# Issuing the stores of the spectral result from ScalarE, with the order of all steps set anew

## The chip, the core and the metric

The kernel runs on one core of a Trainium2 chip. The metric is device time in microseconds (us), the median of several runs. Its engines are TensorE (PE in the profile; its weight loads are PEld), VectorE (DVE), ScalarE (ACT), GpSimd (POOL) and SyncE (SP). SP computes nothing here: it issues DMA transfers, in order. Each engine works through its own list of instructions in order and waits on semaphores for the others.

## The reference

32 images of 56 x 56 places with 96 channels go through two layers. Cut to what matters:

```python
# layer 0: layer norm, product to 192 channels, 3x3 convolution, SiLU, residual
h = layernorm(x);  y = conv3x3(h @ w_in[:, :192]) ;  x = x + silu(y)
# layer 1, first half: spectral mixing over the 3136 places of an image
h = relu(bn1(layernorm(t) @ w1.T))                     # 96 -> 192 channels
X = fft(h, axis=places)
xr = relu(X.real*rd - X.imag*idg + rb);  xi = relu(X.imag*rd + X.real*idg + ib)
t = t + bn2(ifft(xr + 1j*xi).real @ w2.T)              # 192 -> 96 channels
# layer 1, second half: two linear layers with 8-bit floating-point inputs
t = t + q_linear(relu(q_linear(layernorm(t), W1, b1)), W2, b2)
```

## The kernel before, in words

All images go through one long chain of *steps*, and four stages of four neighbouring images run side by side. While an image is in the spectral stage, the next ones are in the convolution and in the first transform, and an older one is in the last two linear layers. Image 19's input is read while image 15's spectral result is on its way back.

The Fourier transform over 3136 places is done as a transform over 56 rows and one over 56 columns, with data turned round between them by way of memory. For each image:

- `fetch`, `take_in`, `make_image`: four chunks of the input (`xl`, three buffers) are loaded (L404), their statistics taken on VectorE (`st_a`, L144), scaled (`xa`, L454) and multiplied into the convolution's input `img` (`im`, L180). `load` reads the same input once more into `t` for the residual (also L404).
- `conv_part` (`cv`, L215 and L219), `conv_tokens` (`st`, L253), `conv_end`: the convolution, turned back to places and added to `t`. `norm_b` takes the statistics of `t` (`st_b`, also L144), `deviation` finishes them, `tokens_a` transposes (`tp_n`, L172).
- `forth` (`ph`, L266), `forth_a` (`pa`, copied to `u` at L280), `store_a`: the product to 192 channels and the first transform. `u` is stored to memory in seven groups, `da<-u` (L506).
- `fetch_a` loads it turned round, `at<-da` (L512). The first three loads of an image wait for the last store of `da`.
- `second` (`px`, L294; ScalarE makes `av` from it, L299 to L301), `second_parts` and `second_relus` (`sv` and `gt` on VectorE, L310 to L320), `second_w2` (`pg`), `second_back` (`pe`, L347, copied by ScalarE to `es`, L349): the second transform, the mixing, the product to 96 channels and the first inverse transform.
- `store_back` stores `es` to memory, `de<-es` (L543): seven calls for an image, each of two DMAs, so 14 for an image and 448 in all. The seventh call is the last unit of an image; it is called es(3,0) below.
- `fetch_y` loads that turned round, `y<-de` (L552). The first of these loads needs all 14 stores. `back` (`py`, L191) and `back_end` do the second inverse transform and add to `t` (L560).
- `normal`, `ffn_start`, `ffn_first` (`pf`, L373, copied to `h` at L375), `ffn_middle` (L379, L383), `ffn_second` (`po`, L393, copied to `y` at L395), `ffn_end` (L400), `store` (`out<-t`, L606): the linear layers.

The order of the steps is written as a list: `plan` gives every step of every image a time, in units of an eighth of an image, and `SHIFT` adds a small correction by step name and arguments. The list is sorted by these times. A scheduler then simulates the program in that order and settles how the instructions of neighbouring steps interleave on each engine. So `SHIFT` decides what stands behind what on every engine and in SP's list.

All these transfers are issued by SP; only four loads at the start come from ScalarE. The completion of transfers is counted by eight semaphores that are used in turn, so a transfer also waits, before it is issued, until the one eight places earlier in the program has landed.

```python
    def store_back(im, m, j0):
        p0, p1 = UNITS[m]
        es = im.held.pop(("es", m, j0))
        rows = im.de[p0:p1].rearrange("(h j) m c -> m h j c", h=2)
        for half in range(2):
            nc.sync.dma_start(rows[:, half, j0 : j0 + 2], es[:, half])
```

Of the kernel before, what the change touches and what calls it, by code (L numbers as in the profile page):

```python
# [50 lines left out]


SHIFT = {
    "back": 0.016, "back_end": -0.049, "conv_end": 0.319, "conv_end:2:1": 0.035, "conv_first": 0.24,
    "conv_first:0": -0.152, "conv_last": 0.284, "conv_part": 0.25, "conv_part:1:0": -1.292, "conv_part:2:1": 0.03,
    "conv_tokens": 0.24, "conv_tokens:0:1": -0.118, "conv_tokens:1": -0.08, "deviation": 0.071,
    "deviation:1": -0.023, "fetch": 0.364, "fetch_a": 0.059, "fetch_a:3": 0.296, "fetch_a:4": 0.619,
    "fetch_a:5": 0.174, "fetch_y": 0.167, "fetch_y:6": 1.932, "ffn_end": -0.036, "ffn_end:5": 0.211,
    "ffn_first": -0.312, "ffn_first:0:1": 0.338, "ffn_first:1": 0.027, "ffn_first:2": 0.021,
    "ffn_first:2:1": -0.304, "ffn_first:3:2": -0.175, "ffn_middle": -0.085, "ffn_middle:1:1": -0.102,  # L60
    "ffn_middle:2": 0.023, "ffn_middle:5": -0.011, "ffn_middle:6": -0.156, "ffn_middle:6:2": 0.223,
    "ffn_second": -0.087, "ffn_second:2": 0.003, "ffn_start": -0.085, "forth": 0.014, "forth:0": 0.016,
    "forth:5:0": 0.224, "forth:5:1": -0.073, "forth_a": 0.013, "load": 0.179, "make_image": 0.24,
    "make_image:0:4": 0.012, "norm_b": 0.24, "normal": 0.071, "normal:1:0": -0.209, "normal:2:2": 0.065,
    "normal:6:0": -0.106, "second": 0.046, "second_back": 0.046, "second_back:0:0": -0.061, "second_back:1": -0.034,
    "second_back:2:2": 0.039, "second_parts:0:0": -0.03, "second_parts:1:0": -0.059, "second_parts:1:2": 0.22,
    "second_parts:2:1": 0.016, "second_parts:2:2": 0.11, "second_relus": -0.027, "second_relus:0:0": 0.092,
    "second_relus:0:1": -0.147, "second_relus:1:1": 0.116, "second_relus:1:2": 0.038, "second_relus:2:0": 0.003,
    "second_w2": 0.046, "second_w2:2": 0.01, "store": -0.085, "store:3": 0.36, "store:4": 0.04, "store:6": -0.25,
    "store_a": 0.016, "store_a:2": 0.657, "store_back": 0.077, "store_back:1:2": -0.126, "store_back:2": 0.123,  # L70
    "take_in": 0.376, "tokens_a": 0.014,
}


# [16 lines left out]
def hybrid_kernel(ctx: ExitStack, tc: tile.TileContext, x, par, spar, cpar, w_in, conv_w, w1, w2, fw1, fb1, fw2, fb2, fa, fb, ib, ia, rows, ones6, out):  # L91
    nc = tc.nc
# [445 lines left out]
    def store_back(im, m, j0):  # L538
        p0, p1 = UNITS[m]
        es = im.held.pop(("es", m, j0))  # L540
        rows = im.de[p0:p1].rearrange("(h j) m c -> m h j c", h=2)
        for half in range(2):
            nc.sync.dma_start(rows[:, half, j0 : j0 + 2], es[:, half])  # L543

    def fetch_y(im, g):
        if g < NG:
# [68 lines left out]
    def plan(b):  # L615
# [76 lines left out]
        for m, (p0, p1) in enumerate(UNITS):  # L692
            both = p1 - p0 > PG
            for at, u in ((0, 0), (0.606, 1), (1.099, 2)) if both else ((0.088, 0), (0.674, 2)):
                at += S0 + SS * m + (0.125 if m + u == 0 else 0)
                put(at, second, m, u)
                put(at + 0.22, second_parts, m, u)
                put(at + 0.47, second_relus, m, u)
            for j0 in range(0, (p1 - p0) // 2, 2):
                at = S0 + SS * m + (2.024 if both else 1.221) + 0.062 * j0  # L700
                put(at, second_w2, m, j0)
                put(at + 0.2, second_back, m, j0)
                put(at + 0.575, store_back, m, j0)
# [338 lines left out]
```

## Time and profile before

| what | value |
|---|---|
| median of 3 runs | 3087.11 us (3083.41 to 3087.77) |
| the profiled execution: its time, its span | 3088.49 us, 3086.4 us |
| busy share of the span: PE, PEld, DVE, ACT, POOL | 95%, 74%, 74%, 72%, 21% |
| mean granted clock of TensorE | 0.965 of full speed |
| bytes moved, mean rate | 363.65 MB, 118 GB/s |
| stores `de<-es` | 448, of 84 KB |
| loads `y<-de` / `at<-da` / `t<-in_x` (large) / `xl<-in_x` (large) | 224 of 168 KB / 224 of 336 KB / 96 of 360 KB / 93 of 360 KB |

"Granted clock" is the share of its full clock that TensorE was allowed at a time. Busy shares are averages: what matters is which wait ends last where TensorE stands idle. In the profile, a row with SPq or ACTq is a DMA instruction on the list of SP or ScalarE: its duration is the time for which it held that list, not the time of the transfer. Times in a view count from the start of the span; one image takes about 93 us, and the views below show the end of the spectral stage of one of them, around 1500 to 1530 us.

### The profile page before, as it was taken

To read this page: it belongs to the slowest core of one execution; us is meant where nothing else is said; L and a number is where in the kernel's file an instruction comes from. 1 tells how busy PE (TensorE), PEld (TensorE's weight loads), DVE (VectorE), ACT (ScalarE), POOL (GpSimd) and SP (SyncE) were. 2 spreads that over 40 slices of the span, in tenths; PEclk is the share of its full clock that TensorE was granted. 3 is DMA by queue.
4 is the path that set the end of the run, shared out by engine and by line. 5 is a ranking of instruction groups with operands and counts; after the bars stand their busy time and mean duration, and the time that the engine had idled before them with its cause. 6 is when DMAs were issued, how large, how long until landed. Compare 5 with 4: busy or idle time off the path is not lost.

```text
span 3086.4 us, 86223 instructions
## 1 busy us (share of the span) xinstructions
PE 2926.7 (95%) x34037; PEld 2298.6 (74%) x34037; DVE 2296.3 (74%) x6704; ACT 2237.1 (72%) x5415; POOL 644.2 (21%) x400
## 2 busy tenths in 40 slices
PE   8899999999999999999999999999999999999986
PEld 6678777778777778777777777777777777777764
DVE  5557777787777777777777777777777877776777
ACT  3467777778777778777777777777777777777876
POOL 2211122222122222122212122212122222121110
PEclk9899999999999999999999999999999999999996
DMA  4544355444354544354544454543455544444442
GB/s 95 148 108 100 100 134 134 125 123 112 99 136 129 128 123 106 105 139 127 128 116 105 116 139 126 129 114 103 120 132 125 127 122 105 119 124 108 111 112 61
DMA packets 500059, 363.65 MB, mean 118 GB/s; under 512 B 346156, under 2 KB 450636, under 8 KB 499428
## 3 DMA queue, kind: packets, MB, share of 16 engines
q1 hardware_dynamic: 497758, 357.39, 45.4%
q8 instruction: 268, 4.39, 0.6%
q10 hardware_dynamic: 1897, 0.76, 0.1%
q14 instruction: 136, 1.11, 0.1%
HBM read 201.13 MB, written 156.89 MB: 116 GB/s over the span
## 4 chain that ended last, share of the span: by engine, by line
PE 69%; DMA 13%; ACT 9%; DVE 7%; issue 1%; SPq 1%; POOL 0%; ACTq 0%; POOLq 0%; DVEq 0%
PE cv L219 12%; PE ph L266 8%; PE px L294 8%; PE pe L347 5%; PE im L180 5%; PE pg L337 4%; PE pa L191 4%; DMA xl<-in_x 4%; PE pg L333 4%; DMA de<-es 4%; PE cv L215 3%; PE py L191 3%; PE pf L373 3%; PE st L253 3%; DMA y<-de 2%; PE po L393 2%
## 5 line engine op out<-in xcount | busy, mean ns | idle before, releaser
L219 PE MATMUL cv<-img,wv 97*32 97x196 f32 x13248 | 658.3, 340 | 0.0
L219 PEld LDWEIGHTS cv<-img,wv 97*32 97x32 f32 x13248 | 427.7, 112 | 121.6
L154 POOL TENSOR_TENSOR rs_c<-var_c,mhalf 120x8 f32<-120x8 f32 (+1 forms) x128 | 209.7, 1639 | 1206.0 <-DVE var_c L152 1202.4
L294 PEld LDWEIGHTS px<-fb_sb,at 112*64 112x64 f32 (+1 forms) x3584 | 327.3, 173 | 121.6 <-issue 49.0
L266 PE MATMUL ph<-w1a,n2t 97*120 97x192 f32 x1792 | 399.1, 346 | 0.0
L268 ACT ACTIVATE h<-ph,rs_b 120x192 f32<-120x192 f32 x896 | 333.3, 432 | 84.2 <-PE ph L266 83.0
L294 PE MATMUL px<-fb_sb,at 112*64 112x112 f32 (+3 forms) x3584 | 388.7, 289 | 5.8 <-ACT y L395 1.9
L266 PEld LDWEIGHTS ph<-w1a,n2t 97*120 97x120 f32 x1792 | 288.6, 187 | 106.3 <-issue 64.0
L375 ACT CAST h<-pf 128x448 f16<-128x448 f32 x672 | 354.2, 554 | 8.4 <-PE pf L373 8.3
L154 POOL TENSOR_TENSOR rs_b<-var_b,mhalf 120x8 f32<-120x8 f32 (+1 forms) x128 | 233.2, 1831 | 537.0 <-DVE var_b L152 523.6
L154 POOL TENSOR_TENSOR rs_a<-var_a,mhalf 120x8 f32<-120x8 f32 (+1 forms) x128 | 198.2, 1550 | 657.4 <-DVE var_a L152 657.4
L180 PE MATMUL im<-rows_sb,xa 120*96 120x168 f32 x1792 | 325.1, 312 | 3.2 <-DVE xa L454 0.5
L379 DVE TENSOR_SCALAR h<-h,b1q 128x448 f16<-128x448 f16 x672 | 219.1, 331 | 107.0 <-ACT h L375 96.2
L312 ACT ACTIVATE sv<-sv 128x224 f32<-128x224 f32 (+2 forms) x352 | 138.8, 394 | 211.8 <-DVE sv L311 211.7
L299 ACT ACTIVATE av<-px,spar_sb 128x224 f32<-128x224 f32 (+2 forms) x352 | 161.0, 457 | 163.4 <-PE px L294 160.5
L180 PEld LDWEIGHTS im<-rows_sb,xa 120*96 120x96 f32 x1792 | 255.2, 164 | 23.9 <-ACT img L185 12.8
L310 DVE SCALAR_TENSOR_TENSOR sv<-px,spar_sb,av 128x224 f32<-128x224 f32 (+2 forms) x352 | 153.4, 436 | 153.5 <-ACT av L301 153.0
L144 DVE BATCH_NORM_STATS2 st_a<-xl 120x6 f32<-120x192 f32 x434 | 142.1, 355 | 163.1 <-DMA xl<-in_x 163.1
L337 PE MATMUL pg<-w2x,gt 128*112 128x96 f32 (+1 forms) x1792 | 246.2, 261 | 0.0
L373 PE MATMUL pf<-n3t,w1q 96*128 96x448 fp8e5 x672 | 231.1, 362 | 15.2 <-ACT n3t L368 7.8
L337 PEld LDWEIGHTS pg<-w2x,gt 128*112 128x112 f32 (+1 forms) x1792 | 244.3, 180 | 0.1
L333 PE MATMUL pg<-w2y,gt 128*112 128x192 f32 (+1 forms) x896 | 234.0, 343 | 4.5 <-DVE gt L320 2.8
(124 smaller groups left out, 6305.2 us busy)
## 6 DMA issues: line engine op xcount, KB each, us to landing
da<-u SPq DMA_DIRECT2D x448, 168.0 KB
at<-da SPq DMA_DIRECT2D x224, 336.0 KB
out<-t SPq DMA_DIRECT2D x224, 180.0 KB
de<-es SPq DMA_DIRECT2D x448, 84.0 KB
y<-de SPq DMA_DIRECT2D x224, 168.0 KB
t<-in_x SPq DMA_DIRECT2D x96, 360.0 KB
xl<-in_x SPq DMA_DIRECT2D x93, 360.0 KB
t<-in_x SPq DMA_DIRECT2D x32, 180.0 KB
```

The costliest lines, as they stand in the source:

```text
L154: nc.gpsimd.tensor_tensor(rs, var, mhalf[:, :n], ALU.pow)
L180: nc.tensor.matmul(ps[:, j], xa[:, t0 + j, :], rows_sb, start=True, stop=True)
L191: nc.tensor.matmul(to, lhs, rhs, start=True, stop=True)
L219: tc.keep_in_program_order(nc.tensor.matmul(*args, start=(dx == 0), stop=(dx == 2)))
L266: nc.tensor.matmul(ph[:, j, :], n2t[:, 2 * j2 + j, :], w1a, start=True, stop=True)
L268: nc.scalar.activation(h[:, j], ph[:, j % 2], AF.Relu, scale=rs[:, j : j + 1])
L294: nc.tensor.matmul(px[rows, j], lhs, fb_sb[:, first(p) : first(p + 1)], start=True, stop=True)
L333: nc.tensor.matmul(pg[:, :, j, :], lhs, w2y, start=True, stop=False, skip_group_check=True)
L337: nc.tensor.matmul(pg[:, half, j, :], lhs, w2x, start=False, stop=True, skip_group_check=True)
L373: nc.tensor.matmul(pf, w1q[:, k * 128 : (k + 1) * 128], n3t, start=True, stop=True)
L375: nc.scalar.copy(h1, pf)
L379: nc.vector.tensor_scalar(h2[:, k], h1, b1q[:, k : k + 1], 0.0, ALU.add, ALU.max)
```

## The change

The two DMAs of `store_back` are issued from ScalarE's list instead of SP's. The table `SHIFT` is replaced by a longer one, made with the assumption that transfers land later; through it the order of all steps changes. No arithmetic, tile or transfer is added or removed. In the new file all lines behind the table stand 12 lower (L543 becomes L555).

```diff
-    "back": 0.016, "back_end": -0.049, "conv_end": 0.319, "conv_end:2:1": 0.035, "conv_first": 0.24,
...
-    "deviation:1": -0.023, "fetch": 0.364, "fetch_a": 0.059, "fetch_a:3": 0.296, "fetch_a:4": 0.619,
-    "fetch_a:5": 0.174, "fetch_y": 0.167, "fetch_y:6": 1.932, "ffn_end": -0.036, "ffn_end:5": 0.211,
...
-    "forth:5:0": 0.224, "forth:5:1": -0.073, "forth_a": 0.013, "load": 0.179, "make_image": 0.24,
-    "make_image:0:4": 0.012, "norm_b": 0.24, "normal": 0.071, "normal:1:0": -0.209, "normal:2:2": 0.065,
...
-    "second_w2": 0.046, "second_w2:2": 0.01, "store": -0.085, "store:3": 0.36, "store:4": 0.04, "store:6": -0.25,
-    "store_a": 0.016, "store_a:2": 0.657, "store_back": 0.077, "store_back:1:2": -0.126, "store_back:2": 0.123,
-    "take_in": 0.376, "tokens_a": 0.014,
+    "back": 0.027, "back_end": -0.049, "back_end:2": -0.057, "conv_end": 0.41, "conv_end:0:1": 0.519,
...
+    "conv_tokens:2:1": -0.249, "deviation": -0.063, "deviation:1": -0.023, "fetch": 0.436, "fetch:3": 0.682,
+    "fetch_a": 0.033, "fetch_a:3": 0.249, "fetch_a:4": 0.619, "fetch_a:5": 0.174, "fetch_a:6": -0.088,
+    "fetch_y": 0.125, "fetch_y:4": 0.481, "ffn_end": -0.001, "ffn_end:2": 0.033, "ffn_end:3": 0.262,
...
+    "forth_a:3": -0.063, "load": -0.208, "load:2": 0.605, "make_image": 0.171, "make_image:0": 0.002,
+    "make_image:0:4": 0.012, "make_image:1:4": -0.429, "make_image:2": 0.06, "make_image:2:4": 0.003,
+    "norm_b": 0.233, "norm_b:0": -0.002, "norm_b:1": 0.517, "norm_b:2": 0.512, "normal": 0.011, "normal:0:0": 0.097,
...
+    "second_w2": 0.075, "second_w2:0:0": -0.023, "second_w2:2": 0.01, "store": -0.222, "store:3": 0.041,
+    "store:4": 0.04, "store:6": -0.25, "store_a": -0.165, "store_a:2": 0.657, "store_a:3": 0.064,
+    "store_back": 0.106, "store_back:0": 0.038, "store_back:1:2": -0.126, "store_back:2": 0.123,
+    "store_back:2:0": -0.125, "store_back:2:2": 0.567, "take_in": 0.236, "tokens_a": 0.075,
+    "tokens_a:3": -0.08,
...
-            nc.sync.dma_start(rows[:, half, j0 : j0 + 2], es[:, half])
+            nc.scalar.dma_start(rows[:, half, j0 : j0 + 2], es[:, half])
```

The instruction lists of the two built programs show what this does at the end of an image's spectral stage. Before, SP's list there reads: last store of `u`, `out`, `xl` chunk 1, three loads `at`, two loads `t`, `xl` chunk 2, the two stores of es(3,0), `out`, `xl` chunk 3, four loads `y`. After, it reads: two `out`, last store of `u`, two loads `t`, three loads `at`, `xl` chunks 1 and 2, `out`, `xl` chunk 3, four loads `y`. The two stores stand in ScalarE's list, each behind one more copy than the one that makes `es`. TensorE's list between `pe` of es(3,0) and `py` has nearly the same work in both. On VectorE, the statistics of `xl` chunk 1 stood ahead of the scaling of the next image's chunk 0 and well ahead of `sv` of the next image's first unit; after, three of their four instructions stand between that scaling and `sv`. Thirteen of the fourteen passes `st_b` stood ahead of `ffn_end` of group 3 on VectorE; after, all fourteen stand behind it.

## The prediction

> **What bounds the kernel now.** I read the page's busy shares first, then TensorE's waits, then SP's list and the chain around the largest wait, then rows by window.
>
> ```profile
> PE 2926.7 (95%) x34037; PEld 2298.6 (74%) x34037; DVE 2296.3 (74%) x6704; ACT 2237.1 (72%) x5415; POOL 644.2 (21%) x400
> ...
> PE py L191 <- DMA y<-de: 81.9, 31, 3.9
> PE ps_wt L751 <- DMA win<-in_w_in: 8.1, 1, 8.1
> PE st L253 <- ACT s L245: 8.1, 29, 1.4
> ```
>
> TensorE is the bound: 95% busy, no other engine above 74%. Of its waits (us in total, times, longest) only one is large: `py` waits 31 times for `y`, 81.9 us, so 2.64 us for an image. All others are below 0.3 us for an image. One image of the 31 (SP's rows, then the chain, each with start and duration):
>
> ```profile
> 1507.62 4.66 SPq L404 DMA_DIRECT2D xl<-in_x  x1
> 1512.33 0.90 SPq L543 DMA_DIRECT2D de<-es  x2
> 1513.32 0.50 SPq L606 DMA_DIRECT2D out<-t  x1
> ...
> 1518.03 2.01 SPq L552 DMA_DIRECT2D y<-de  x4
> ```
>
> ```profile
> 1508.71 0.47 ACT es L349
> ...
> 1512.77 5.21 DMA de<-es
> ...
> 1518.40 3.47 DMA y<-de
> ```
>
> The last `es` is ready at 1509.18, but its two stores stand in SP's list behind an `xl` load whose issue alone held the list 4.66 us. They go out at 1512.33, 3.15 us late; the landing takes 5.21 us, `y` another 3.47, and `py` starts at 1521.91 after a gap of 3.29 us. The gap has a second price:
>
> ```profile
> 1505.00:1509.00 4.00, 4.00 (x43) 3.97 (x42) 1.99 (x8) 2.61 (x7) 0.91 (x2) 1.00 0.94 271
> 1509.00:1514.00 5.00, 5.00 (x42) 4.91 (x39) 3.89 (x8) 4.68 (x13) 1.28 (x1) 1.00 1.12 197
> 1514.00:1517.00 3.00, 3.00 (x44) 2.49 (x46) 0.45 (x2) 3.00 (x10) 0.00 (x0) 1.00 1.02 263
> 1518.62:1521.91 3.29, 0.00 (x0) 0.00 (x0) 3.29 (x13) 0.00 (x0) 0.58 (x1) 1.00 0.68 192
> 1522.00:1529.00 7.00, 7.00 (x60) 4.24 (x64) 5.31 (x16) 2.75 (x7) 1.98 (x2) 0.51 0.65 184
> ```
>
> The three columns at the end are granted clock, DMA share and GB/s. Behind the gap the clock is 0.51 for 7 us. Behind two gaps of 2.20 us I found 0.72 (1708 to 1714) and 1.00 (2452 to 2458): a gap of that size may or may not cost the clock. From 216 to 2820 us, the steady part with 28 images, the mean clock is 0.98: 0.02 x 2604 = 52 us lost, 1.9 us for an image. So 2.64 + 1.9 = 4.5 us of an image hang on `y`. Also seen: before the gap the DMA engines are full (share 0.94 to 1.12).
>
> **The change part by part**, for one image, against the profiled 3088.49 us (1.4 above the median).
>
> A, the stores leave SP. They can go at 1509.7, behind the copy that follows `es` in ScalarE's list (ended 1509.65). With the old landing, 5.21 us, and 0.9 us for the two issues, `de` is complete at 1515.8. By then SP must also have come to its `y` loads; a first `y` issued at 1516 lands 3.8 us later, near 1519.8. Alone, this leaves 1.2 us of the 3.29; but TensorE arrives later too (C, D, E: 3.1 us in this image), at 1521.7. So the wait for `y` goes: -2.64. It stays at its old size if ScalarE's issue is stuck as SP's was.
>
> B, the clock. If the gap breaks into pieces of 2.1 us and less, most of the 1.9 comes back; the two gaps of 2.20 us say that some pieces still cost it. Bounds 0 and 1.9; I take three quarters, -1.4.
> [...]
>
> C, given back on VectorE. In the new order two `t` loads and three `at` loads stand ahead of chunk 1 of `xl`, and three of the four `st_a` of that chunk stand ahead of `sv` of the next image's first unit. In the old order this chunk was issued at 1503.11, ahead of `at`, and its `st_a` ran at 1506.89. Counted in the trace's packets, `t` (1920 packets at 440 for a us) takes 4.4 us, `at` (336 at 80) 4.2, `xl` (120 at 80) 1.5: 10.1 us from about 1504.2, and 0.8 us to the wake-up: 1515.1. Three `st_a` (0.89) and three `sv` passes (1512.92 to 1514.09, 1.17) make 1517.1. `px_0_1` on TensorE, which needs the buffer that the third pass frees, ran at 1515.00. So TensorE stands 2.1 us; scaled by 2.64 / 3.29 for a mean image +1.7. Bounds: 0, if `t` gets out 2 us sooner; 2.6, if the 2.09 MB go at 197 GB/s, the lowest full-share row above (10.6 us).
>
> D, `st_b` later. `deviation` must be done before `tp_n` in the middle of TensorE's work there. Its last steps cost VectorE 0.61 us for POOL's `rs_b` and 0.17 of its own (1505.59): between 0, if other work covers it, and 0.8; I take the middle, +0.4.
>
> E, fourteen issues on ScalarE. SP's rows of this form have a median of 0.447 us; ScalarE's own at the start of the kernel took 0.23 to 0.67. All 14: 6.3 us of ScalarE, which is idle for 28% of 93 us. The pair of es(3,0) delays `av` by 0.9 us, where ScalarE was busy 4.68 of 5.00, but `sv` waits longer for `xl` there (C covers it; uncovered, the whole 0.9 would count). Of es(1) four stand in a row, 1.8 us; the 10 us around them (1560 to 1570) had 1.18 idle on ScalarE, so 0.6 is left. Bounds 0 and 1.8; +0.6. Queued behind each issue are `img`, `h` and `av` copies, for which TensorE waits through PSUM. All lane waits of these stores but one are long satisfied; that one, the second store of es(3,0), waits for the first `t` load, eight places earlier, whose packets are served first (done at 1504.2 + 2.2): no cost if `t` starts as in C.
>
> The other moved steps exchange neighbours on engines with 26% to 28% idle and keep TensorE's list nearly the same between `pe` and `py`: 0 taken; below nothing too, since the small waits of TensorE, some 60 us in all, may shrink or grow by a third (20 us either way).
>
> Sum: -2.64 - 1.4 + 1.7 + 0.4 + 0.6 = -1.34 us, times 31 = -42. 3088.5 - 42 = 3047, on the scale of the median 3046. Its own range, with C at 0 to 2.6 and the 20 us: 3010 to 3080.
>
> **The rivals.** (1) *All of it gained*: nothing of C, D, E reaches TensorE, as in the image above the old waits for VectorE and ScalarE were near zero. -2.64 - 1.9 = -4.54, times 31 = -141: 2946. For it: stores 3 us earlier are nearly the whole gap. Against it: A alone leaves 1.2 us, and without TensorE's delay `y` would still be late. Chance 0.13.
>
> (2) *Slower: ScalarE is held by its own issue.* The 4.66 us row shows that an issue can hold its list while the DMA engines are full (1.12 from 1509 to 1514). If SP's and ScalarE's issues share what is full, the first store, reached at 1509.7, goes when SP's did, at 1512.28: 2.6 us in which ScalarE stands, with `h`, `img` and `av` behind it; the second adds some 0.4. TensorE runs dry (it had no slack in `img` and `px`): +3.0 in place of C, +0.4 and +0.6 as before, `y` -2.64, and the clock is lost as now. +1.36 times 31 = +42: 3129. It decides once the two rows of es(3,0) hold ScalarE over 0.9 + 1.34 = 2.2 us for an image. For it: SP's row; against it: SP's list may have been stuck in a limit of its own, and the store is small beside `xl`. Chance 0.35.
> [...]
>
> (3) *No change*: the bytes ahead are the same, the engines are full until 1517, so `de` and `y` land when the backlog is through, whoever issues; the gap moves to other instructions and the clock drops as before. 3080 to 3100. For it: shares of 0.94 to 1.12; against it: from 1518.62 the share is 0.68, so the end of the gap is latency. Chance 0.16, half of it within 0.2%.
>
> **How the numbers follow.** Forecast 0.36, rivals 0.13, 0.35, 0.16. 0.2% (6 us) is what a measurement of this kernel can tell. Faster: 0.36 + 0.13 + 0.03 of rival 3 = 0.52; same 0.08; slower 0.35 + 0.05 = 0.40. Range: it leaves out half of rival 1 (below 2960) and a third of rival 2 (C on top of the held issue, above 3140), 0.18 together: 2960 to 3140. The forecast's own range is 3010 to 3080.
>
> **What would show it.** In the waits of TensorE, `py` for `y` should fall from 81.9 to below 20 us (A). The granted clock from 216 to 2820 us should be 0.99 or more (B). New waits: `px` for `sv` some 50 us, with VectorE's `st_a` held by `xl` ahead of it (C); `tp_n` some 12 us (D). ScalarE's issue rows should be near 0.45 us each (E); pairs of 2 us or more in front of `av` show rival 2. If `py` still waits 50 us with short issues, rival 3 holds. I am wrong in the mechanism if `py` waits less and another wait on TensorE, not named here, is over 30 us.

## The result, and the profile after

The changed kernel takes 3095.2 us (median of 5 runs, 3088.7 to 3104.3) against 3087.1 before: 1.0044 times, 95% interval 1.0026 to 1.0063, so slower by 0.4% and not faster. The forecast was 3046.

```profile
PE 2952.1 (96%) x34037; PEld 2299.8 (74%) x34037; DVE 2306.0 (75%) x6704; ACT 2261.1 (73%) x5415; POOL 616.7 (20%) x400
```

Busy time of the engines after: TensorE is busy 25 us longer for the same instructions. Its waits:

```profile
PE px L306 <- DVE sv L325: 51.0, 29, 2.9
PE py L203 <- DMA y<-de: 12.3, 8, 3.9
```

`py` waits 12.3 us in place of 81.9, as forecast; `px` waits 51.0 for `sv`, also as forecast. The image that matches the one shown of before, first in SP's list, then in ScalarE's:

```profile
1502.49 0.95 SPq L416 DMA_DIRECT2D t<-in_x  x2
1503.87 1.46 SPq L524 DMA_DIRECT2D at<-da  x3
1505.38 0.88 SPq L416 DMA_DIRECT2D xl<-in_x  x2
...
1517.30 1.60 SPq L564 DMA_DIRECT2D y<-de  x4
```

```profile
1508.40 0.48 ACT L361 COPY es<-pe 112x384 f32<-112x384 f32 x1
...
1508.91 0.31 ACTq L555 DMA_DIRECT2D de<-es  x1
...
1509.29 0.44 ACTq L555 DMA_DIRECT2D de<-es  x1
```

ScalarE issues the first of the two stores 0.03 us behind the last `es`; the issues take 0.31 and 0.44 us. Yet SP issues `y` only at 1517.30, when `de` is complete: 7.6 us behind the end of the stores' issues, where it had been 4.8. It is the landing that `y` waits for: the last of the second store's landing signals comes at 1517.25 (before: 1517.98, and `y` at 1518.03), while the counting semaphore that this `y` takes had been free since 1511.73. What the DMA engines did meanwhile is seen by queue, SP's (q1), then ScalarE's (q10): packets, MB and share of the engines' time from 1509 to 1513.5:

```profile
q1 hardware_dynamic: 419, 1.12, 95.6%
...
q10 hardware_dynamic: 30, 0.01, 1.0%
```

Of the 480 packets of the two stores 30 were served in these 4.5 us; the other 450 follow from 1513.5 to 1517.5. The chain of waits of the same stretch:

```profile
1505.38 10.16 DMA xl<-in_x
...
1515.84 0.61 DVE st_a L156 x2
1516.44 0.35 DVE sv L322
1516.80 0.36 DVE sv L323
1517.16 0.37 DVE sv L325
...
1517.58 0.48 PE px L306 x2
```

The `xl` load takes 10.16 us from its issue, then come the passes of VectorE. The rows by window (granted clock, DMA share and GB/s at the end):

```profile
1505.00:1509.00 4.00, 4.00 (x43) 3.90 (x42) 3.40 (x16) 2.84 (x7) 3.42 (x3) 1.00 1.17 205
1509.00:1514.00 5.00, 5.00 (x39) 4.91 (x38) 3.38 (x8) 4.72 (x13) 2.40 (x2) 1.00 0.98 255
1515.02:1517.58 2.56, 0.00 (x1) 0.00 (x1) 2.02 (x7) 0.70 (x3) 0.00 (x0) 1.00 0.60 171
1518.00:1524.00 6.00, 6.00 (x68) 3.73 (x67) 5.67 (x18) 2.94 (x8) 3.86 (x2) 0.72 0.64 160
```

The gap is now ahead of `px` (2.56 us), and the clock falls behind it as before. To see where the time is, each profiled span is split into TensorE's *idle* time (span minus busy), its *clock loss* ((1 - mean granted clock) x span) and the *rest* (busy minus clock loss: work at full clock, with whatever stalls the records count as busy; idle time at half clock is in both of the others). The clock has three digits, so the last two are good to about 1.5 us. These columns are of one profiled run each, and the clock differs from run to run. Every run has its span and mean clock on record, so *runs* gives the clock loss as the mean of a kernel's runs (lowest to highest), then the mean of the time without it, span x clock, which differs by 1 to 5 us (one standard deviation) between runs of one kernel. `y` is when SP issues the first `y`, counted from the end of the last `es` copy, the mean of 26 images of the middle; *gap* is the idle time just ahead of `py`, likewise. *Runs* leaves out three slow runs of e2 (over 1.5% above its fastest); without them its median is 3084.9.

| profile | median us (ratio, 95%) | idle | clock loss | rest | y | gap | runs: clock loss; time without |
|---|---|---|---|---|---|---|---|
| before | 3087.1 | 159.7 | 108.0 | 2818.7 | 8.26 | 2.68 | 100 (83 to 127); 2982 |
| changed | 3095.2 (1.0026 to 1.0063) | 137.7 | 111.2 | 2840.9 | 7.97 | 0.17 | 111 (102 to 121); 2983 |
| e1 engine only | 3101.9 (1.0031 to 1.0065) | 175.5 | 83.7 | 2840.9 | 6.97 | 1.75 | 84 (77 to 90); 3014 |
| e2 order only | 3090.0 (0.9990 to 1.0047) | 137.6 | 88.6 | 2829.0 | 8.24 | 0.23 | 113 (89 to 130); 2968 |
| e3 changed, t later | 3154.8 (1.0199 to 1.0259) | 191.9 | 148.1 | 2812.0 | 5.71 | 3.87 | 150 (138 to 168); 3004 |
| e4 before, t later | 3140.1 (1.0163 to 1.0198) | 176.2 | 150.7 | 2812.2 | 4.39 | 2.25 | 148 (144 to 154); 2991 |
| e9 control | 3131.5 (1.0128 to 1.0194) | 168.4 | 150.6 | 2818.8 | 8.49 | 2.84 | 139 (128 to 151); 2991 |
| e10 narrow fill | 3172.4 (1.0242 to 1.0349) | 167.2 | 155.9 | 2859.3 | 8.35 | | 150 (133 to 172); 3022 |
| e13 wide fill | 3191.8 (1.0303 to 1.0399) | 193.3 | 120.7 | 2863.3 | | | 143 (121 to 164); 3049 |
| e14 before, wide fill | 3107.5 (1.0049 to 1.0095) | 160.8 | 58.7 | 2872.5 | 8.38 | | 66 (59 to 75); 3037 |
| e11 st_a behind sv | 3160.7 (1.0175 to 1.0294) | 143.2 | 189.5 | 2825.9 | 8.10 | 2.28 | 184 (163 to 193); 2970 |
| e12 t later, order kept | 3111.3 (1.0067 to 1.0130) | 157.1 | 120.9 | 2822.8 | 4.45 | 0.89 | 132 (114 to 157); 2979 |
| e15 t and xl later | 3215.0 (1.0392 to 1.0455) | 221.3 | 164.5 | 2839.0 | 2.96 | 0.06 | 154 (144 to 164); 3061 |
| e16 e12, more st_a later | 2989.8 (0.9685 to 0.9738) | 103.8 | 53.8 | 2830.0 | 4.50 | 0.97 | 53 (48 to 54); 2938 |
| e17 e16 from ScalarE | 3034.0 (0.9820 to 0.9874) | 137.7 | 45.4 | 2843.5 | 4.62 | 0.92 | 53 (45 to 58); 2979 |

Changed against before, from the profiles: idle -22.0, clock loss +3.2, rest +22.2: +3.4 us (spans 3086.4 and 3089.8; the medians are 8 apart). Over all runs (before: 52, measured beside the experiments) the clock loss is 11 higher and the time without it the same, 2982 and 2983: what left as idle time came back as rest. So the questions are: why `y` did not come earlier, why the clock did not recover, and what the rest is. Line numbers in the profiles of experiments are shifted by their own edits.

### The profile page after: what moved, and what is told of

Same layout as the page of the kernel before. It is cut to its first block, busy times and chain, and to the rows that moved or that the text cites. A ratio compares the mean times of both kernels' runs of the same rounds, so it can differ in the third digit from the quotient of the medians.

```text
span 3089.8 us, 86135 instructions
## 1 busy us (share of the span) xinstructions
PE 2952.1 (96%) x34037; PEld 2299.8 (74%) x34037; DVE 2306.0 (75%) x6704; ACT 2261.1 (73%) x5415; POOL 616.7 (20%) x400
## 3 DMA queue, kind: packets, MB, share of 16 engines
q8 instruction: 268, 4.39, 0.6%
## 4 chain that ended last, share of the span: by engine, by line
PE 75%; DMA 11%; DVE 7%; ACT 4%; issue 1%; ACTq 0%; SPq 0%; POOL 0%; DVEq 0%; POOLq 0%
PE cv L231 15%; PE px L306 9%; PE ph L278 9%; DMA xl<-in_x 7%; PE pa L203 5%; PE pg L349 5%; PE pe L359 5%; PE pg L345 4%; PE cv L227 4%; PE pf L385 4%; PE py L203 3%; PE im L192 3%; PE po L405 3%; PE tp_n L184 2%; PE st L265 2%; DMA de<-es 1%
## 5 line engine op out<-in xcount | busy, mean ns | idle before, releaser
L166 POOL TENSOR_TENSOR rs_c<-var_c,mhalf 120x8 f32<-120x8 f32 (+1 forms) x128 | 220.1, 1720 | 1309.0 <-DVE var_c L164 1303.4
L166 POOL TENSOR_TENSOR rs_b<-var_b,mhalf 120x8 f32<-120x8 f32 (+1 forms) x128 | 189.4, 1498 | 713.1 <-DVE var_b L164 649.5
L166 POOL TENSOR_TENSOR rs_a<-var_a,mhalf 120x8 f32<-120x8 f32 (+1 forms) x128 | 205.0, 1603 | 408.6 <-DVE var_a L164 403.2
L197 ACT COPY img<-im 96x336 f32<-96x336 f32 x448 | 190.1, 441 | 61.5 <-PE im L192 48.1
L292 ACT COPY u<-pa 128x768 f32<-128x768 f32 x224 | 181.4, 810 | 72.8 <-PE pa L206 64.2
```

The lines of the kernel that those rows point to most:

```text
L166: nc.gpsimd.tensor_tensor(rs, var, mhalf[:, :n], ALU.pow)
```

## The experiments

**e1 and e2, the two halves alone.** e1 is the kernel before with the stores on ScalarE, e2 the changed kernel with the stores on SP:

```diff
-            nc.sync.dma_start(rows[:, half, j0 : j0 + 2], es[:, half])
+            nc.scalar.dma_start(rows[:, half, j0 : j0 + 2], es[:, half])
```

> The stores of es issued by ScalarE, with the old table SHIFT (only the first half of the change). Theory T1 (the bytes ahead decide): in the changed kernel the stores of es(3,0) went out 3 us earlier than before, but landed only 0.7 us earlier (1517.3 against 1518.0), because the DMA engines were full. So here too py should still wait for y, some 1.9 us in place of 2.64 for an image (60 us in all), the clock still falls, no px wait for sv: 3060 to 3085 us. Theory T2 (the new issuer gains, the new order loses it): py waits under 0.8 us for an image, and the clock recovers: 3000 to 3040 us. Theory T3 (the issues of ScalarE cost TensorE): over 3095 us.

> The new table SHIFT, with the stores issued by SP as before (only the second half of the change). In SP's list the stores then stand behind two t, three at and two xl loads. T1: px waits for sv as in the changed kernel (about 51 us), py waits for y in addition by the little that the stores land later, up to 1 us for an image: 3095 to 3130 us. T2: the px wait and the whole old wait for y add up: 3140 to 3170 us.

Waits of TensorE, e1, then e2:

```profile
PE py L191 <- DMA y<-de: 53.7, 31, 4.3
PE pg L333 <- ACT gw L339: 21.9, 28, 0.8
```

```profile
PE px L306 <- DVE sv L325: 49.7, 27, 2.9
PE py L203 <- DMA y<-de: 19.2, 11, 5.4
```

e1: `y` is issued 1.3 us earlier and `py` waits 28 us less, a third of what was hoped (T1). But `pg` waits for `gw` 28 times, once for nearly every image, which is new, and idle time rises by 16 and the rest by 22. So the wait is T1's, and the time, with T3's price on top, is T3's. e2: the `px` wait and the small `py` wait are there with SP's stores: the order makes them, not the issuer. And SP, too, issues the first store 0.03 us behind the last `es` there (2.20 before): the new order alone frees the stores, and `y` comes at 8.24 all the same. With SP the median is 5 us below the range of T1 and within the interval of no change; T2 is out by 50 us. In both comparisons of the issuer the rest is higher with ScalarE (e1 22 above before, changed 12 above e2); over all runs the time without clock loss is 32 and 15 higher.

**e3 and e4, the loads of `t` behind `y`** (e3 in the changed kernel, e4 in the one before; `t` is first used some 35 us after it lands):

```diff
-            in_turn(self.chunk(i)[:, :, :C], self.tokens[:, j0:j1, :], self.b < 3)
+            in_turn(self.chunk(i)[:, :, :C], self.tokens[:, j0:j1, :], True)
     # SHIFT: "load:0": 0.8, "load:1": 0.4 in e3; "load:0": 0.6 in e4
```

> The changed kernel with the loads of t (half 0) moved behind the y loads in SP's list; the loads in_x are kept in the order of the step list for all images, which also puts xl chunk 3 behind the first four y loads. t is first used some 30 us later, so nothing should wait for it. T1: 720 KB (4.4 us of the DMA engines) less are ahead of xl chunk 1 and of the stores: px waits for sv under 0.5 us for an image, py for y under 1 us, the clock falls at fewer places: 2980 to 3030 us. T2 expects only the px wait to go, 1.65 x 31 = 51 us, and the y wait to come back for part: 3040 to 3080 us.

> The kernel before (stores issued by SP, old SHIFT) with the same two moves of loads: t (half 0) and xl chunk 3 behind the y loads. T1: SP's list is no longer held 4.66 us by the xl load, de lands some 4 us earlier, the wait of py for y falls from 2.64 us below 0.8 us for an image, and most of the clock loss goes: 2985 to 3035 us, without ScalarE's help. T2 (the issuer is what matters): the wait for y stays over 1.5 us for an image: 3050 to 3087 us.

Both are slower, though the step that was aimed at works: `y` is issued at 5.71 and 4.39 us in place of 7.97 and 8.26, with either issuer. The time went elsewhere, for two reasons. First, the scheduler takes `y` to land sooner and puts `cv`, `px` and `pf` behind `py`: TensorE comes to `py` at 5.66 us (12.62 in the changed kernel) and 6.88 (9.31 before). Second, VectorE: in e3 SP's list ahead of `y` holds an `out` store that waits for VectorE,

```profile
1547.12 0.35 SPq L620 DMA_DIRECT2D out<-t  x1
1547.58 1.70 SPq L566 DMA_DIRECT2D y<-de  x4
```

which had stood on `st_a` for `xl` until 1544.8; in e4 chunk 2 of `xl` is awaited ahead of `hq`:

```profile
PE py L192 <- DMA y<-de: 69.9, 31, 3.8
PE po L394 <- DVE hq L384: 35.4, 32, 1.7
```

and in both the clock loss is some 40 us above that of before. (With `st_a` behind `sv`, in e12 below, `po` no longer waits for `hq`.) So these two runs tell of the landing, not of the whole sum.

**e6 to e8, `py` listed later** (e6 before, e7 with `t` later, e8 that with the stores on ScalarE):

```diff
+    "back:0": 0.6, "back_end:0": 0.3,   # e6: 0.75, and conv_part:0:0 -0.2
```

> The kernel before, with the first py of an image listed later (back:0 and back_end:0 in SHIFT): on TensorE one pa and half a ph, some 1.3 us of work, and all of cv's first block stand ahead of py. Loads and stores as before, from SP. The gap of 2.68 us should shrink to about 1.4 us. Theory W: windows over half idle become rare, the steady clock loss of 57 us falls under 20: idle -40, clock -40, 3000 to 3025 us. Rival V: only the idle time goes, 3040 to 3055 us. Rival (VectorE and the linear layers then wait for py): 3070 us or more.

> The kernel before (stores from SP) with the loads of t behind y and py later on TensorE. In the run with the loads alone y was issued 4.39 us behind the last es copy (8.26 before) and py could start at 9.13 (12.00 before), but TensorE also came to py earlier (6.88 against 9.31), since the order of steps moved cv behind py; here that is put back. If the loads ahead are what matters, no wait for y is left (TensorE at 10.6, y at 9.1), the wait of po for hq (35 us) stays: 2990 to 3020 us. If the t loads only collide elsewhere (da, at), other waits of 40 us or more appear: 3050 to 3090 us.

> The same two moves with the stores issued by ScalarE. With no wait for y left in either, the difference is ScalarE's issuing alone: in the old order it added 44 us of waits and 19 us of slower TensorE work (engine change alone against before), so 30 to 60 us above the kernel with SP's stores: 3030 to 3070 us. If the issuer costs nothing: equal within 10 us.

Measured 3208.7, 3129.4 and 3197.6 us. In these three the first `py` of an image stands in the list behind the load of the third `y` chunk into the same buffer, and so it computes with that chunk and waits for that load. Nothing is drawn from them. In the runs below `py` is listed ahead of that load, with `cv` moved instead.

**e5, e9, e10, e13, e14: what makes the clock fall.** In the clock records of all profiles the half-clock stretches begin on a fixed grid of 3.413 us (before and changed: every change of the clock lies within 5 ns of it). TensorE's idle share was counted in each window of that grid, over all 19 profiles. At full clock, a window idle for under 0.2 was followed by half clock 3 times in 14619; 0.2 to 0.4: 23 in 687; 0.4 to 0.5: 110 in 223; 0.5 and more: 428 in 431. At half clock, a window idle for 0.1 or more was followed by another one 402 times in 405, and even one with less than 0.02 idle 376 times in 888. e5 fills the gap of e3 with six matmuls of 57 rows and 64 columns:

```diff
+        if q == 0 and b:   # e13, e14: lhs fb_sb[:, :128], all 112 rows, 2 matmuls
+            for _ in range(6):
+                tc.keep_in_program_order(nc.tensor.matmul(to, ia_sb[: HW + 1], spare, start=True, stop=True))
         together(products)
```

> As the kernel with the loads of t moved in the changed kernel (3154.8 us, gap of 3.87 us ahead of py in each image, 37 clock drops that cost 124 us of full clock), with six idle-time matmuls (57x384 from constants, overwritten by the first real one) on TensorE some 25 instructions ahead of py: about 2.4 us of filling work, which adds nothing to the result. Theory W (in the runs so far the clock fell after a 3.41 us window of a fixed grid that was over half idle, and never after one under 0.3): the gap shrinks to about 1.5 us, nearly no window is half idle, some 25 of the 37 drops go: 3070 to 3100 us, although TensorE does more work. Rival V (the clock follows the wait for y or the small matmuls behind it, not the idle share): drops stay, 3150 to 3165 us. Rival U (the fillers delay what y or its neighbours need): over 3170 us.

3316.3 us (1.0726 to 1.0790). The six took 4.08 us, not 2.4, `pa` now waits 82.5 us for `t += py`, and the loss did not fall (192 over its runs). But ten windows with 0.1 to 0.4 idle time now led to half clock, and in nine of those the narrow matmuls filled 0.68 to 0.86: width seemed to count. So e9 fixes TensorE's list around `py` as a control, e10 adds two narrow matmuls to it, e13 two wide ones (112 rows, 128 columns) of the same length, and e14 puts the two wide ones in the order of before.

> Control for the next run: the kernel before with the first two blocks cv of an image listed just ahead of and behind its first py, so that TensorE's list around py is fixed (cv block, py, cv block, pa). Loads, stores and all work as before. The gap ahead of py stays near 2.7 us, the steady clock loss near 57 us: 3070 to 3110 us. It is here to be compared with the next run, not with the kernel before.

> The control with two matmuls (57x384, from constants, 1.36 us by the rows of the earlier filled run) ahead of the first py of each image, into the PSUM tile that py overwrites: TensorE's list is otherwise the same, so TensorE only does 31 x 1.36 = 42 us more work, in time in which it waited for y. Theory W (the clock falls after a window of 3.41 us on a fixed grid that is over half idle): the gap becomes 1.3 us, hardly a window is half idle, the steady clock loss falls from about 57 to under 20 us, and the kernel is 25 to 50 us faster than the control for doing more. Rival V (the clock falls for another reason, as the wait or the narrow matmuls behind it): as the control within 10 us. Rival U (the fillers are in the way): slower by up to 42 us.

> As the control with two filling matmuls ahead of py (3172 us; 57 rows, 64 columns), but the two filling matmuls are wide: 112 rows, 128 columns, the same 384 elements, so the same time on TensorE. Theory W2 (the clock follows the use of the array over a window, and narrow matmuls count as part idle): the loss at half clock falls from 140 us to below 95: 3095 to 3135 us. Theory W1 (idle time alone counts): no change, 3155 to 3190 us. Theory V (the clock has nothing to do with the gap): as W1, with the same 37 drops.

> The kernel before with the two wide filling matmuls (1.36 us) ahead of the first py of an image, and TensorE's list otherwise as before: 42 us more work in the gaps of 2.68 us. W2: gaps of 1.3 us, the loss at half clock falls from 98 to about 45 us, while t += py on VectorE comes a little later (up to 15 us): 3035 to 3070 us, faster than before with more work. W1 and V: 3085 to 3130 us.

Clock loss in the profiles: control 150.6, narrow fill 155.9, wide fill 120.7. But the wide fill was profiled in the fastest of its four runs; over all runs the three are 139, 150 and 143 and overlap. So these runs don't show that either fill, or its width, lowers the loss here. The time of e13, 3191.8, is at the top of W1's range and far from W2's: `pa` waits 82 us there (59 with the narrow fill, 10 in the control). What does show the width is the windows. Take those at full clock with 0.1 to 0.4 idle and at least 0.3 of fill: with narrow matmuls (e5, e10) 14 of 24 led to half clock, with wide ones (e13, e14) none of 27. In e14 the loss falls from 108.0 to 58.7 in the profiles (busy time alone: 98 to 49, with 45 expected) and from 100 to 66 over all runs; windows at least half idle fall from 27 to 8. Its TensorE rows ahead of `py`, and span and clock:

```profile
1519.08 1.56 PE L367 MATMUL py<-fb_sb 112*128 112x384 f32 x4
1521.12 0.53 PE L193 MATMUL py<-y,ia_sb 57*64 57x384 f32 x1 [0.48 <-DMA y<-de]
```

```profile
core 0: 3092.0 us, clock 0.981
```

A filled gap cost less clock here: that much is shown, though no run has e14's list without the fill. The gain is not shown, since the fill (rest +54 us) is not free: `t += py` came later, `pa` waits 28.8 us for it, and the idle time stays at 160.8.

**e11, the `px` wait undone.** The changed kernel; the `st_a` passes of `xl` chunk 1 go behind `sv`, all else in the same order:

```diff
+        if i in (1,) and im.b - 3 in thirds:          # thirds[b]: third sv pass of the first unit
+            with tc.issue_after(thirds[im.b - 3]):
+                _, _, rs = stats(xl, "a", im.b, i)
```

> The changed kernel with one thing undone: the st_a passes of xl chunk 1 are issued on VectorE behind the third sv pass of the next image's first unit. TensorE's list around py, SP's and ScalarE's lists are those of the changed kernel. The wait of px for sv (51 us) goes in every theory. T1 (the gap only moved): de still lands some 8 us behind the last es, y some 4 to 5 us later, TensorE now comes to py 2.5 us sooner, so py waits some 2 us for an image again (50 to 75 us): 3075 to 3100 us. T2 (the px wait was the loss of this change): py waits under 0.8 us for an image, 3010 to 3045 us.

```profile
PE py L203 <- DMA y<-de: 69.9, 32, 4.3
```

T1: the `px` wait has gone from the list, and `py` waits for `y` 69.9 us again, within 12 us of before, with the stores on ScalarE. Idle time is 143.2, nearly as in the changed kernel. That the time is 65 us worse is the clock: a loss of 189.5 against 111.2 (184 against 111 over all runs). The clock falls 36 times, about as often as before (34), but stays at half for 10.6 us each time in place of 6.4, and T1's range did not have that. What stands behind the gap differs between the two; which part of it keeps the clock low was not tested.

**e12, e15, e16, e17: without the wait.** e12 is e4 with `cv` and `py` put back and `st_a` of chunks 2 and 3 behind `sv`; e15 moves all `xl` loads to the middle of the image instead; e16 is e12 with `st_a` of chunk 3 and of the next chunk 0 behind `t += py`; e17 is e16 with the stores on ScalarE.

```diff
+    "load:0": 0.6, "back:0": 0.39, "forth_a:0": 0.09,   # and conv_part(0, 0) 0.47 earlier
+        behind = {1: None, 2: thirds.get(im.b - 3), 3: added.get(im.b - 4), 0: added.get(im.b - 5)}[i]
```

> The kernel before, stores from SP, with the t loads (half 0) behind the y loads as in the earlier run (3140 us), but with the two side effects of that run undone: the st_a passes of xl chunks 2 and 3 stay behind sv on VectorE (so that hq and sv don't wait for xl), and the first py is listed later, so that po and px stay ahead of it (cv stands behind it). y should be issued 4.4 us behind the last es copy and py be possible at 8.2 to 9.1; TensorE should come to py at 7.3 to 9.3: a gap of 0.5 to 1.5 us in place of 2.68, under half a window. If bytes ahead of the stores are the bound of before: 2995 to 3030 us. If the t loads collide with da and at later: other waits of 40 us or more, 3060 us or more.

> The kernel before, stores from SP, with all loads of t and xl kept in the order of the step list: t (half 0) behind the y loads and all chunks of xl in the quiet middle of an image, so that only three at loads stand ahead of the stores of es(3,0), and VectorE has no st_a near py. py is listed later (cv's first block still falls behind it). If the bytes ahead are the bound: y is issued within 4.4 us of the last es copy, TensorE comes at about 7.2 and y at 8.0, a gap under 1 us; pa no longer waits for t (51 us in the earlier run): idle 160 to 110 us, loss at half clock 98 to 60: 2990 to 3045 us. If the moved loads collide with da and at: im waits for xl, or px for at, 40 us or more: over 3070 us.

> As the run with t later and the order kept (3111 us), with one thing more: the st_a passes of xl chunk 3 and of the next image's chunk 0 are issued on VectorE behind t += py of the first chunk. pa's wait for t (51 us) should fall below 10, with no wait of TensorE of over 2 us per image left: idle 157 to about 115 us. If the clock follows the gaps: loss at half clock 107 to 60 us; 3000 to 3035 us, the first kernel here that beats the kernel before. If VectorE then only waits elsewhere (sv, hq): another wait of 30 us or more, 3070 us or above.

> The same with the stores of es issued by ScalarE; TensorE's list around py is the same. In the run before SP issued the stores 0.03 us behind the last es copy, since nothing holds its list there, so the issuer has nothing to gain. If ScalarE's 14 issues cost as in the engine-only run (63 us of waits and slower TensorE work for 31 images): 25 to 60 us above the run with SP. If they are hidden: equal within 10 us. If the issuer itself matters for the landing: faster by 20 us or more.

e12: `y` as expected (4.45, gap 0.89), but a new wait, VectorE's rows and what TensorE makes of them:

```profile
1519.02 0.36 DVE L147 BATCH_NORM_STATS2 st_a<-xl 120x6 f32<-120x192 f32 x1 [2.84 <-DMA xl<-in_x]
...
1520.93 0.95 DVE L571 TENSOR_TENSOR t<-py,t 120x768 f32<-120x768 f32 x1
```

```profile
1521.93 0.53 PE L194 MATMUL pa<-h,fa_sb 56*64 56x384 f32 x1 [2.16 <-DVE t L571]
```

e15: with only the three `at` ahead, SP issues `y` 2.96 us behind the last `es`, and the gap is gone (0.06). The moved loads collide as the last line of its expectation said, only elsewhere: `st` waits 117.8 us for `s`. e16: waits of TensorE, then the chain at the end of one image:

```profile
PE py L194 <- DMA y<-de: 34.2, 30, 3.9
PE pf L380 <- ACT n3t L375: 8.9, 10, 1.5
```

```profile
1552.19 0.32 SPq L555
...
1552.56 4.53 DMA de<-es
...
1557.48 4.30 DMA y<-de
```

2989.8 us, 0.9711 of before: the fastest kernel here, with the stores on SP. No wait took the old one's place, and the gap of about 1 us is under half a window; the clock loss halves, 100 to 53 over all runs. e17 is 44 us slower; the profiles show idle +33.9, rest +13.5 and clock -8.4, and over all runs the clock loss is the same (53) and the time without it 42 higher. Its waits of TensorE have two lines that e16 has not:

```profile
PE pg L340 <- ACT gw L346: 21.8, 28, 0.8
...
PE im L183 <- ACT img L188: 9.9, 28, 1.4
```

With nothing holding SP, the issuer has nothing to give, and ScalarE's 14 issues cost 1.4 us for an image.

## Why the prediction was wrong, step by step

Two steps failed, A's landing and B. B is where the time went: 46 of the 49 us between forecast and result. The two hang together: as `y` did not come earlier, TensorE had to be late for the wait to go, and so the gap moved instead of breaking into small pieces.

- **A, the stores leave SP (-2.64).** The wait fell as said (by 2.25 for an image), but not by the step given. The step that failed is "with the old landing, 5.21 us": issued 2.2 us earlier, the stores stood behind more bytes (in the image shown 1.63 MB of other transfers were served between the end of their issues and the landing, 0.87 before), and the time from the end of their issues to `y` grew from 5.09 to 7.07 us, so that `y` was issued 0.3 us earlier. `py` stopped waiting because TensorE came 3.3 us later, which C, D and E had foreseen (3.1). e11 takes C away and the wait is back; e1 prices the issuer at 28 us of it; e15, e12 and e4 show the backlog as the cause, with SP issuing (`y` at 2.96, 4.45 and 4.39 us, 8.26 before). In the stretch from 1509 to 1513.5 SP's queue had 95.6% of the engines' time and ScalarE's 1.0%. Why is open.
- **B, the clock (-1.4).** Failed: -43 us were taken, +3 measured (+11 over all runs). The step is "if the gap breaks into pieces of 2.1 us and less, most of the 1.9 comes back". A window of 3.41 us that is idle for 0.4 to 0.5 (1.4 to 1.7 us) was followed by half clock about every second time (110 in 223), and one idle for more nearly always (428 in 431); of the 37 gaps over 0.3 us between 216 and 2820 us, 23 are longer than 1.5. The clock fell 28 times in place of 34, but for 7.9 us each time in place of 6.4. The "two gaps of 2.20 us" that the step was judged by are windows of that width; the gaps in them are 2.17 and 2.09 us. So half a window idle was enough here, and of the windows filled with narrow matmuls 14 of 24 led to half clock with 0.1 to 0.4 idle.
- **C, given back on VectorE (+1.7).** Right: 52.7 us taken, 51.0 measured; in the image shown `px` at 1517.58 where 1517.1 was worked out, and by the chain named.
- **D (+0.4).** Too large: `tp_n` waits 2.0 us for `t` in all, not 12.
- **E (+0.6, 19 us).** Of the right size in the new order (rest +12, idle 0 from e2 to the changed kernel; 15 over all runs), too small elsewhere (32 in e1, 42 in e17). It hardly shows as idle time of TensorE in the new order. Rival 2 fell: the longest issue row is 1.56 us, the median 0.40.
- **The other steps (0).** Order alone makes the rest 10 us longer and the idle time 22 shorter (before to e2); over all runs the time without clock loss falls by 14 and the clock loss rises by 13.

The forecast's own range, 3010 to 3080, is narrower than its terms: C at 0 and at 2.6 with 20 us either way give 2973 to 3094, and 3095.2 was measured.

Rival 3, "the gap moves to other instructions and the clock drops as before", 3080 to 3100, is what happened, by the cause given there. It got 0.16; against it stood the DMA share of 0.68 behind 1518.6, read from the stretch in which `y` itself was under way and not from the one ahead of it.

## What to carry to other kernels

When a store waits behind other transfers, ask how many bytes are ahead of it before asking who issues it (here `t` loads behind `y`, with the statistics set later, gave `y` at 4.50 us and 2989.8 us in all with SP's stores, e16; ScalarE's stores alone gave 6.97 and 3101.9, e1); move a load that is needed late, and hold the order of the other engines while doing so. Here the gain was lost where VectorE, working in order, waited for a load of `xl` with something urgent behind it (`px` waits 51.0 us in the changed kernel, `po` 35.4 in e4, `pa` 51.3 in e12): follow each urgent step back through its own list. And price a gap of TensorE by its length against the window that the clock records show (3.41 us here), not by its microseconds alone.

## What was not expected of the hardware

- The clock changed on a fixed grid of 3.41 us: behind a window at least 0.5 idle it fell nearly always (428 in 431), behind one under 0.2 nearly never (3 in 14619), and it stayed low behind windows at least 0.1 idle (402 in 405). What else kept it low behind windows almost without idle time (376 in 888 under 0.02) is open.
- Matmuls of 57 rows and 64 columns did not hold the clock as wide ones did: 14 of 24 windows filled with them led to half clock, none of 27 with 112 rows and 128 columns (0.1 to 0.4 idle, at least 0.3 filled).
- Packets of ScalarE's queue waited while SP's were served: 30 of 480 in 4.5 us, 1.0% of the engines' time against 95.6%.
- The run-to-run spread of one program went with the clock: two of e2's runs took 3057 us at a mean clock of 0.971 and 3099 at 0.958; 0.013 x 3080 = 40 of the 42 us. A clock loss read from a single run can mislead by as much (e13).
- A kernel with 49 us more of matmuls, the fill, lost 34 us less to the clock (e14 against before, all runs).
